# A two-layer graph kernel: the last 255 keys split over both halves of the PE array, key moments from every other row tile, and a narrower test of the candidate pieces

## The chip, the cores and the metric

The kernel runs on one core of one Trainium2 chip. The time is the device time of one execution in microseconds (us), as the median of three runs. Five engines work side by side, each on its own list of instructions in order: PE (TensorE, matmuls; its weight loads are listed as PEld), DVE (VectorE), ACT (ScalarE), POOL (GpSimd) and SP (SyncE, which here only issues transfers). They wait for one another through semaphores.

## The reference, cut to what matters

There are 3327 nodes with 256 features and a sparse weighted adjacency matrix. Layer 0 does two steps of message passing along two ways and adds them up; layer 1 is a graph attention over the neighbours. The change lies in layer 0's learned attention, which keeps for each node the largest probabilities that together make 0.9:

```python
def _top_p_attention(X, W1, W2, W3):
    q = X @ W1.T @ W2.T
    k = X @ W3.T
    logits = q @ k.T / TAU
    probs = jax.nn.softmax(logits, axis=-1)
    idx = jnp.argsort(-probs, axis=-1)
    sp = jnp.take_along_axis(probs, idx, axis=-1)
    cs = jnp.cumsum(sp, axis=-1)
    keep_sorted = cs - sp < TOP_P
    ...
    A = probs * mask
    return A / jnp.maximum(A.sum(-1, keepdims=True), 1e-12)
...
for n in range(STEPS):          # STEPS = 2
    A = _top_p_attention(Xa, W1, W2, W3)
    Xf = R @ Xf                 # R: adjacency plus identity, rows divided by their sums
    Xa = A @ Xa
    Z = Z + Xf @ U1[n].T + Xa @ U2[n].T
```

Everything is float32; queries and keys have 64 features.

## The kernel before

The nodes are cut into 26 row tiles of 128 (the last has 127 rows). Two programs are in the kernel. `fast` computes everything under assumptions that it tests at the end; `general` is a slower program that runs afterwards only if a test failed for some row (`bad`, `far`, `again`).

**Keys and queries.** Since a key has 64 features, the keys of one row tile fill only half of the 128 partitions. `half_of` gives a tile its half (`t // 4 % 2`) and its columns in `kt`: groups of four tiles alternate between the halves. `logits(k)` makes 1024 logits of a row tile at a time, 512 on each half of the PE array, as two matmuls (line 845); `k` runs from 0 to 3, and the fourth piece holds the 255 keys that are left, all on the lower half. `exps` (line 856) takes the exponentials on ACT with their sums. The tile `e` has 3328 columns; POOL writes a zero in the last one for each row tile (line 833).

**Moments.** To guess the threshold of a row, the kernel needs mean and variance of its logits. They come from the sum of the keys and of their products, `gk` (64 x 65 on each half). `moments` adds one row tile to it: a PE transpose of the keys (`turn`, line 733), an ACT copy into `kk` (line 737), a PE product with 65 columns (line 742) and two DVE adds (line 754). `keys_summed` puts this chain into the plan; it is called for every row tile in `prepare` (step 0's keys) and in `finish1` (step 1's keys). `gk` is divided by the number of keys (line 1675), and `stats` (lines 769 to 807) makes mean and variance for each row.

**Search.** For each row tile: `guess` gives a first threshold, `count` (line 893, ACT, over all 3327 exponentials) and `step` (POOL, once on DVE in step 1) improve it two or three times, `window` (lines 948 and 953, DVE) takes the eight largest values below an upper bound out of each of 16 pieces of 208, `sort` and `choose` find among these candidates the exact place of the cut, and `drop` (line 1003) clears what lies under the threshold. `attention` then transposes `e` (line 1016), copies it (line 1021) and multiplies (line 1028). `full` is the product with the adjacency matrix (line 1060), whose tiles SP loads into four buffers.

**The test.** `met` holds numbers for each row tile: 0 the sum, 1 the largest of the eighth values of the pieces, 2 how many values of the window are kept, 3 the first value left out, 4 a count of ties. A row fails in `failures` (lines 1337 to 1348) if, among other things, some piece's eighth value is not below the first value left out, since then that piece might hide a ninth that counts.

**Order.** Nothing is run in the order of the source. `Plan.put` takes each piece of work with its engine, an estimated length, a rank, what it needs and which buffers it takes and gives back; `Plan.order` simulates the engines with these lengths and always takes the ready piece of lowest rank, and `issue` writes the instructions out in that order, which then is fixed for each engine. In the preparation POOL turns variances into factors (lines 672 to 675) and copies keys into `kt` (line 1127); ACT applies the relu (line 1104) and copies projections (lines 1123, 1124); PE transposes (line 1109), projects keys and queries (line 1117) and multiplies the sources of the adjacency products (`project_u`, line 1155), which ACT and DVE copy out (lines 1158, 1159). A piece of SP, `spread`, stores step 1's keys as they come, and `fetch_keys` loads them back.

Of the kernel before, what the change touches and what calls it, by code (L numbers as in the profile page):

```python
# [10 lines left out]
F32 = mybir.dt.float32  # L11
# [4 lines left out]
ALU = mybir.AluOpType  # L16
# [3 lines left out]
P = 128  # L20
N = 3327
NT = 26
NP = NT * P
D = 256
DA = 64
# [545 lines left out]
def fast(  # L571
# [18 lines left out]
    V, S, T, GP = nc.vector, nc.scalar, nc.tensor, nc.gpsimd  # L590
# [19 lines left out]
    bad = const.tile([P, STEPS, NT], F32, name="bad")  # L610
# [6 lines left out]
    for k, v in enumerate(QUANTILE[1:3]):  # L617
        GP.memset(adds[:, k : k + 1], v)

    def half_of(t):  # L620

        r = t // 4 % 2
        lo = t // 8 * 512 + t % 4 * P
        return slice(r * DA, r * DA + DA), slice((1 - r) * DA, (2 - r) * DA), slice(lo, lo + P)

    with ExitStack() as l0:
        wpool = l0.enter_context(tc.tile_pool(name="wpool", bufs=1))
        small = l0.enter_context(tc.tile_pool(name="small", bufs=2))
# [10 lines left out]

        c = wpool.tile([P, NT, D], F32, name="c")  # L640

        kt = wpool.tile([P, 4 * 512 - 256], F32, name="kt")
        qq = wpool.tile([P, NT, P], F32, name="qq")

        kks = [wpool.tile([P, P + 2], F32, name=f"kk{k}") for k in range(2)]
        for kk in kks:
            GP.memset(kk[:, :: P + 1], 1.0)
        wqk = wpool.tile([P, 2, 2, P], F32, name="wqk")
# [7 lines left out]

        stat = wpool.tile([P, 2, NT], F32, name="stat")
        sig, zadd, cn, cs = (wpool.tile([P, NT], F32, name=n) for n in ("sig", "zadd", "cn", "cs"))
        met = wpool.tile([P, 5, NT], F32, name="met")
        GP.memset(met, 1.0)  # L660

        def measure(src):
# [61 lines left out]

        def moments(t, kq, ps_k, ps_g):

            r, p = t // 4 % 2, min(P, N - t * P)
            half = slice(r * DA, r * DA + DA)
            held = {}

            def turn():
                held["ps"] = ps_k()
                T.transpose(held["ps"][:, :P], kq(), ident)

            def copy():
                kk = held["kk"] = kks[t % 2]
                S.copy(kk[:, 1 : P + 1], held["ps"][:, :P])

            def product():
                kk = held["kk"]  # L740
                ps = held["ps"] = ps_g()
                T.matmul(
                    ps[:, : DA + 1], kk[:p, 1 : P + 1], kk[:p, r * (DA + 1) : (r + 1) * (DA + 1)], start=True, stop=True
                )

            def gather():
                for to, src in (
                    (gk[half, :DA], held["ps"][half, 1 - r : DA + 1 - r]),
                    (gk[half, DA : DA + 1], held["ps"][half, DA * r : DA * r + 1]),
                ):  # L750
                    if t in (0, 4):
                        V.tensor_copy(to, src)
                    else:
                        V.tensor_add(to, to, src)

            return turn, copy, product, gather
# [59 lines left out]
        class Row:  # L816


            NAMES = (
                "b v w t0 t1 t2 u g k2 p0 p1 p2 p3 j0 j1 j2 j3 r0 s0 s1 s2 B0 B1 B2 q d dt least up h0 h1 room K zs nxt cnt m "  # L820
                "tk rec".split()
            )

# [3 lines left out]
            def open(self):  # L827
                self.e = epool.tile([P, NP], F32, name="e")
                self.sc = small.tile([P, len(self.NAMES)], F32, name="sc", bufs=BUFS["sc"])
                for k, name in enumerate(self.NAMES):  # L830
                    setattr(self, name, self.sc[:, k : k + 1])
                self.s = met[:, 0, self.i : self.i + 1]
                GP.memset(self.e[:, N:], 0.0)

            def logits(self, k):

                if k == 0:
                    self.open()
                pl = ps_l.tile([P, 2, 512], F32, name="pl")
                w = min(1024, N - 1024 * k)  # L840
                for r in range(2):
                    m = min(512, w - 512 * r)
                    if m > 0:
                        half = slice(r * DA, r * DA + DA)
                        T.matmul(  # L845
                            pl[:, r, :m],
                            qq[half, self.i, :],
                            kt[half, 512 * k : 512 * k + m],
                            start=True,
                            stop=True,  # L850
                        )
                self.pl[k] = pl.rearrange("p r w -> p (r w)")[:, :w]

            def exps(self, k):
                pl = self.pl.pop(k)
                S.activation(  # L856
                    self.e[:, 1024 * k : 1024 * k + pl.shape[1]],
                    pl,
                    AF.Exp,
                    accum_out=(self.p0, self.p1, self.p2, self.p3)[k],  # L860
                )
# [232 lines left out]
        def prepare(t, load):  # L1094
# [19 lines left out]
            def project():  # L1114
                ps = held["ps"] = ps_x.tile([P, P], F32, name="px")
                for k in range(2):
                    T.matmul(
                        ps, wqk[:, k, t // 4 % 2, :], c[:, t, k * P : (k + 1) * P], start=(k == 0), stop=(k == 1)
                    )

            def share():
# [7 lines left out]
            def double():  # L1129
# [9 lines left out]
            a = plan.put("ACT", 0.55, r, share, needs=[a], take=["kq"], give=["px"])  # L1139
            k = plan.put("POOL", 0.35, r, keys, needs=[a])  # L1140
            q = plan.put("SP", 0.2, r, double, needs=[a])
            g = keys_summed(
                t, lambda: held["kq"], lambda: ps_a.tile([P, P], F32, name="acca"),
                lambda: ps_a.tile([P, DA + 1], F32, name="accf"), r, [a], ("acca", "accf"), [],
            )
            plan.put("SP", 0.02, r, lambda: None, needs=[k, q, g], give=["kq"], lag=0.0)
            return [k, q], g

# [13 lines left out]
        def finish1(row, done, rank):  # L1162
# [15 lines left out]
            def project():  # L1178
                ps = held["ps"] = ps_x.tile([P, P], F32, name="px")
                for k in range(2):  # L1180
                    T.matmul(ps, wqk[:, k, t // 4 % 2, :], held["xt"][:, k, :], start=(k == 0), stop=(k == 1))

            def share():
                held["kq"] = small.tile([P, P], F32, name="kq", bufs=BUFS["kq"])
# [37 lines left out]
            if direct:  # L1222
# [2 lines left out]
                    plan.put("POOL", 0.4, r, queries, needs=[a, drawn[0]]),  # L1225
                ]
            kq.append(plan.put("SP", 0.3, r, spread, needs=[a, drawn[0] if direct else None]))
            g = keys_summed(
                t, lambda: held["kq"], lambda: ps_x.tile([P, P], F32, name="px"),
                lambda: ps_x.tile([P, DA + 1], F32, name="px"), r, [a, guessed[0]], ("px", "px"), [],  # L1230
            )
            plan.put("SP", 0.02, r, lambda: None, needs=[kq, g], give=["kq"], lag=0.0)
            a = plan.put("PE", 1.75, r + 0.1, project_u2, needs=[x_], take=["px"])
            a = plan.put("ACT", 0.56, r + 0.1, stage, needs=[a], take=["ystage"], give=["px", "xt"])
# [4 lines left out]
        def fetch_keys():  # L1239
            for r in range(2):  # L1240
                half = slice(r * DA, r * DA + DA)
                w = max(half_of(t)[2].stop for t in range(LAST + 1) if t // 4 % 2 == r)
                nc.sync.dma_start(kt[half, :w], kts[half, :w])
            nc.sync.dma_start(qq[:, : LAST + 1, :], qqs[:, : LAST + 1, :])

# [85 lines left out]
        def failures(n):  # L1331

            b, one = bad[:, n], small.tile([P, NT], F32, name="one", bufs=1)
            W = WIN[n]
            V.tensor_scalar(b, met[:, 2], W / 2, None, ALU.subtract)
            V.tensor_mul(b, b, b)
            V.tensor_scalar(b, b, (W / 2 - 0.5) ** 2, None, ALU.is_gt)
            V.tensor_tensor(one, met[:, 1], met[:, 3], ALU.is_ge)  # L1340
            V.tensor_add(b, b, one)
            V.tensor_scalar(one, met[:, 4], 0.0, None, ALU.not_equal)
            V.tensor_add(b, b, one)
            V.tensor_scalar(one, met[:, 0], 1e-25, None, ALU.is_ge)
            V.scalar_tensor_tensor(one, met[:, 0], 1e30, one, ALU.is_le, ALU.mult)
            V.scalar_tensor_tensor(b, one, 0.0, b, ALU.is_equal, ALU.add)

            V.scalar_tensor_tensor(b[:, NT - 1 :], ident[:, P - 1 :], 0.0, b[:, NT - 1 :], ALU.is_equal, ALU.mult)

        def search(row, rank, keys, stats_of, fresh):  # L1350
# [4 lines left out]
            for g in range(2):  # L1355

                def logits(g=g):
                    row.logits(2 * g)
                    row.logits(2 * g + 1)

                a = plan.put(
                    "PE", 2.1 - 0.5 * g, rank - 2.5, logits, needs=[keys, fresh, a], take=["pl", "pl"] + ["e", "sc"] * (1 - g)
                )
                for k in (2 * g, 2 * g + 1):
                    got.append(
                        plan.put("ACT", 1.15 if k < 3 else 0.5, rank - 2.5, row.exps, k, needs=[a], give=["pl"])
                    )
# [303 lines left out]
        for n in range(STEPS):  # L1671
            base = 30.0 * n
            scaled = plan.put(
                "DVE", 0.2, base - 50.0,
                lambda: V.tensor_scalar(gk[:, : DA + 1], gk[:, : DA + 1], 1.0 / N, None, ALU.mult), needs=[sums],
            )
            cuts = (0, 3, NT // 2, NT)
            of = {}
# [104 lines left out]
```

## Time and profile before

| | |
|---|---|
| median of 3 runs | 2272.42 us (2270.28 to 2273.19) |
| profiled execution | 2271.77 us, its span 2269.9 us |
| PE busy | 2207.6 us, 97% of the span |
| DVE, ACT, POOL busy | 1618.2, 1480.0, 915.3 us |
| granted PE clock, mean | 0.992 |

The span runs from the first to the last instruction of the profiled execution. Preparation takes some 60 us, the row tiles of step 0 the time to about 905 us, those of step 1 the time from there to about 1780, and layer 1's attention the rest. A row of the profile names the line of the kernel, the engine and the tiles written and read (`pl<-kt,qq`). A float32 matmul shows up as two records[...].

### The profile page before, as it was taken

To read this page: it belongs to the slowest core of one execution; us is meant where nothing else is said; L and a number is where in the kernel's file an instruction comes from. 1 tells how busy PE (TensorE), PEld (TensorE's weight loads), DVE (VectorE), ACT (ScalarE), POOL (GpSimd) and SP (SyncE) were. 2 spreads that over 40 slices of the span, in tenths; PEclk is the share of its full clock that TensorE was granted. 3 is DMA by queue.
4 is the path that set the end of the run, shared out by engine and by line. 5 is a ranking of instruction groups with operands and counts; after the bars stand their busy time and mean duration, and the time that the engine had idled before them with its cause. 6 is when DMAs were issued, how large, how long until landed. Compare 5 with 4: busy or idle time off the path is not lost. (4 is left out here: it accounts for less than half of the span.)

```text
span 2269.9 us, 36125 instructions
## 1 busy us (share of the span) xinstructions
PE 2207.6 (97%) x11956; PEld 1547.5 (68%) x11956; DVE 1618.2 (71%) x4273; ACT 1480.0 (65%) x2849; POOL 915.3 (40%) x2263
## 2 busy tenths in 40 slices
PE   7999999999999999999999999999999999999997
PEld 5477778777877778877878777878788433343332
DVE  5576656557565562277878898678776898989895
ACT  5766686677666851478887877777872646565553
POOL 6455555546533540256646656665561000000000
PEclk9999999999999999999999999999999999999998
DMA  3011221212212222531222122222222443434341
GB/s 98 20 37 53 83 69 53 64 51 61 74 48 74 69 82 76 183 86 54 65 57 73 56 61 70 70 75 75 67 74 78 119 118 107 120 106 120 102 126 42
DMA packets 189653, 176.96 MB, mean 78 GB/s; under 512 B 14866, under 2 KB 145808, under 8 KB 189328
## 3 DMA queue, kind: packets, MB, share of 16 engines
q1 hardware_dynamic: 187472, 173.30, 26.3%
q8 instruction: 96, 1.57, 0.3%
q10 hardware_dynamic: 1984, 1.26, 0.2%
q14 instruction: 101, 0.83, 0.1%
HBM read 157.66 MB, written 15.89 MB: 76 GB/s over the span
## 5 line engine op out<-in xcount | busy, mean ns | idle before, releaser
L1028 PE MATMUL acca<-rhs,et 128*128 128x256 f32 x2704 | 621.2, 380 | 0.8 <-ACT et L1021 0.8
L893 ACT ACTIVATE junk<-e,sc 128x3327 fp8e5<-128x3327 f32 x182 | 559.1, 3072 | 59.1 <-POOL sc L938 57.8
L1028 PEld LDWEIGHTS acca<-rhs,et 128*128 128x128 f32 x2704 | 498.5, 190 | 63.8 <-ACT et L1021 2.6
L1060 PE MATMUL accf<-main,at 128*128 128x257 f32 x1352 | 314.0, 382 | 4.9 <-DMA at<-in_adjt_dram 4.6
L1060 PE MATMUL accf<-c,at 128*128 128x256 f32 x1352 | 313.4, 382 | 4.8 <-ACT f L1067 4.7
L1535 DVE SCALAR_TENSOR_TENSOR e<-c,low,et 128x832 f32<-128x832 f32 x288 | 289.0, 1076 | 16.3 <-ACT e L1605 9.7
L1060 PEld LDWEIGHTS accf<-c,at 128*128 128x128 f32 x1352 | 250.2, 190 | 54.8 <-issue 14.1
L1060 PEld LDWEIGHTS accf<-main,at 128*128 128x128 f32 x1352 | 250.7, 191 | 47.1 <-issue 8.2
L1021 ACT COPY et<-px 128x512 f32<-128x512 f32 (+1 forms) x364 | 193.6, 553 | 133.3 <-PE acca L1028 72.5
L948 DVE SCALAR_TENSOR_TENSOR y<-e,sc 128x1664 f32<-128x1664 f32 x104 | 206.6, 1987 | 96.3 <-POOL sc L935 63.8
L953 DVE MAX8 cands<-y 128x8 f32<-128x208 f32 x832 | 242.7, 361 | 3.7
L1003 DVE SCALAR_TENSOR_TENSOR e<-e,thr 128x832 f32<-128x832 f32 x208 | 212.6, 1080 | 1.7
L1551 PE MATMUL pl<-e,main 128*64 128x416 f32 x1152 | 212.0, 516 | 0.1
L856 ACT ACTIVATE e<-pl 128x1024 f32<-128x1024 f32 x208 | 179.1, 863 | 45.6 <-PE pl L845 45.3
L1016 PE MATMUL px<-ident,e 128*128 128x128 f32 x1352 | 193.5, 275 | 7.6 <-ACT et L1021 4.5
L1524 ACT ACTIVATE et<-at 128x512 bf16<-128x512 f32 (+1 forms) x208 | 114.5, 550 | 127.6 <-DVE e L1535 82.4
L1016 PEld LDWEIGHTS px<-ident,e 128*128 128x128 f32 x1352 | 160.4, 141 | 51.6 <-issue 12.5
L845 PE MATMUL pl<-kt,qq 64*128 64x512 f32 (+1 forms) x728 | 184.1, 588 | 0.1
L1551 PEld LDWEIGHTS pl<-e,main 128*64 128x64 f32 x1152 | 79.8, 137 | 122.2 <-issue 102.2
L1535 DVE SCALAR_TENSOR_TENSOR rhs<-c,low,et 128x832 f32<-128x832 f32 x128 | 129.2, 1073 | 0.0
L845 PEld LDWEIGHTS pl<-kt,qq 64*128 64x128 f32 x728 | 70.9, 185 | 82.3 <-issue 76.5
L1523 ACT ACTIVATE at<-at 128x512 f32<-128x512 f32 (+1 forms) x208 | 112.1, 539 | 4.3 <-DMA at<-in_adjt_dram 4.2
(486 smaller groups left out, 2834.3 us busy)
## 6 DMA issues: line engine op xcount, KB each, us to landing
at<-in_adjt_dram SPq DMA_DIRECT2D x416, 256.0 KB, 2.7
at<-in_adjt_dram SPq DMA_DIRECT2D x104, 192.0 KB, 3.0
at<-in_adjt_dram SPq DMA_DIRECT2D x52, 128.0 KB, 2.1
ys<-ystage SPq DMA_DIRECT2D x26, 256.0 KB, 2.2
rhs<-in_x_dram SPq DMA_DIRECT2D x26, 128.0 KB, 2.9
ystage<-in_x_dram SPq DMA_DIRECT2D x26, 128.0 KB, 2.0
base<-ys SPq DMA_DIRECT2D x26, 128.0 KB, 2.2
x1s<-ystage SPq DMA_DIRECT2D x26, 128.0 KB, 1.7
```

The lines of the kernel that those rows point to most:

```text
L845: T.matmul(pl[:, r, :m], qq[half, self.i, :], kt[half, 512 * k : 512 * k + m], start=True, stop=True,)
L856: S.activation(self.e[:, 1024 * k : 1024 * k + pl.shape[1]], pl, AF.Exp, accum_out=(self.p0, self.p1, self.p2, self.p3)[k],)
L893: S.activation(junk[:, :N], self.e[:, :N], fn, bias=t, scale=-1.0, accum_out=dst, saturate=False)
L948: V.scalar_tensor_tensor(self.y[:, : hi - lo], self.e[:, lo:hi], self.up, self.e[:, lo:hi], ALU.is_lt, ALU.mult, accum_out=(self.h0, self. ...
L953: V.max(self.cands[:, o // PIECE, :], self.y[:, o - lo : min(o + PIECE, hi) - lo])
L1003: V.scalar_tensor_tensor(piece, piece, self.thr[:, o : o + 1], piece, ALU.is_gt, ALU.mult)
L1016: T.transpose(pt[:, k, :], self.e[:, j * P : (j + 1) * P], ident)
L1021: S.copy(self.et[g][:, :m, :], self.pt.pop(g)[:, :m, :])
L1028: T.matmul(self.acc, et[:, j - 4 * g, :], rhs[self.n][:, j, :], start=(j == 0), stop=(j == NT - 1))
L1060: T.matmul(self.acc[:, : self.w], self.at[j // JC][:, j % JC, :], self.src[:, j, : self.w], start=(j == 0), stop=(j == NT - 1),)
L1535: V.scalar_tensor_tensor(held["e"][:, k, :], extra["both"][b % 2][:, k, :], low[:, j, k : k + 1], held["mask"], ALU.max, ALU.mult,)
L1551: T.matmul(q["acc"][a][k * FH : (k + 1) * FH, c, :C], main[:, j, h * FH : (h + 1) * FH], held["e"][:, h, c * C : (c + 1) * C], start=(j == 0),
```

## The change

- The last row tile goes to the other half (`side`), so that of the last 255 keys 128 lie on the lower half and 127 on the upper one. The fourth piece of `logits` becomes two matmuls of 128 and 127 columns, and a third one with a single column, of constants (`none`), gives the last place the logit -32000, whose exponential is zero. The zero that POOL wrote into `e` is left out.
- The moments are summed over the 13 row tiles of even number alone, in both steps, and divided by their 1664 keys.
- The test of a piece fails a row if the eighth value is above the first one left out, or equals it while `m`, the number of ties kept, isn't zero. For this `m` moves into `met`.
- The planner's length for the second half of a row's logits is 1.4 instead of 1.6.

```diff
+    def side(t):
+        return 1 if t == NT - 1 else t // 4 % 2
     def half_of(t):
-        r = t // 4 % 2
-        lo = t // 8 * 512 + t % 4 * P
+        r = side(t)
+        lo = t // 8 * 512 + (t % 4 * P if t < NT - 1 else 0)
...
+        none = wpool.tile([P, P + 2], F32, name="none")
+        GP.memset(none, 0.0)
+        GP.memset(none[DA : DA + 32, :P], 1.0)
+        GP.memset(none[DA : DA + 32, P:], -1.0e3)
...
             def copy():
-                kk = held["kk"] = kks[t % 2]
+                kk = held["kk"] = kks[t // 2 % 2]
...
-                GP.memset(self.e[:, N:], 0.0)
+                self.m = met[:, 5, self.i : self.i + 1]
...
-                w = min(1024, N - 1024 * k)
+                w = 512 if k < 3 else P
                 for r in range(2):
-                    m = min(512, w - 512 * r)
-                    if m > 0:
-                        half = slice(r * DA, r * DA + DA)
-                        T.matmul(pl[:, r, :m], qq[half, self.i, :], kt[half, 512 * k : 512 * k + m], ...)
-                self.pl[k] = pl.rearrange("p r w -> p (r w)")[:, :w]
+                    m = min(w, N - 1024 * k - w * r)
+                    half = slice(r * DA, r * DA + DA)
+                    T.matmul(pl[:, r, :m], qq[half, self.i, :], kt[half, 512 * k : 512 * k + m], ...)
+                    if m < w:
+                        T.matmul(pl[:, r, m:w], none[half, :P], none[half, P : P + w - m], start=True, stop=True)
+                self.pl[k] = pl[:, :, :w]
...
-            g = keys_summed(
+            g = t % 2 == 0 and keys_summed(
...
-            )
+            ) or None
...
-            V.tensor_tensor(one, met[:, 1], met[:, 3], ALU.is_ge)
+            V.tensor_tensor(one, met[:, 1], met[:, 3], ALU.is_gt)
+            V.tensor_add(b, b, one)
+            V.tensor_tensor(one, met[:, 1], met[:, 3], ALU.is_equal)
+            V.tensor_scalar(two, met[:, 5], 0.0, None, ALU.not_equal)
+            V.tensor_mul(one, one, two)
             V.tensor_add(b, b, one)
...
-                    "PE", 2.1 - 0.5 * g, rank - 2.5, logits, ...
+                    "PE", 2.1 - 0.7 * g, rank - 2.5, logits, ...
...
-                lambda: V.tensor_scalar(gk[:, : DA + 1], gk[:, : DA + 1], 1.0 / N, None, ALU.mult), needs=[sums],
+                lambda: V.tensor_scalar(gk[:, : DA + 1], gk[:, : DA + 1], 1.0 / (NT // 2 * P), None, ALU.mult), needs=[sums],
```

## The prediction, made before the changed kernel was run

> **What bounds the kernel now.** I read the page first, then a table by stretches of time, then the PE timeline of single stretches, and the list of waits last.
>
> ```profile
> span 2269.9 us, 36125 instructions
> PE 2207.6 (97%) x11956; PEld 1547.5 (68%) x11956; DVE 1618.2 (71%) x4273; ACT 1480.0 (65%) x2849; POOL 915.3 (40%) x2263
> ...
> 0.00:60.00 60.00, 44.43 (x256) 33.51 (x256) 31.75 (x130) 34.77 (x114) 36.14 (x123) 0.97 0.35 101
> 60.00:120.00 60.00, 54.49 (x164) 24.11 (x166) 31.31 (x121) 43.46 (x90) 28.90 (x72) 1.00 0.03 10
> 120.00:620.00 500.00, 499.28 (x2489) 395.76 (x2488) 316.67 (x951) 344.65 (x616) 266.19 (x632) 1.00 0.21 62
> 1000.00:1400.00 400.00, 392.03 (x1935) 313.74 (x1934) 334.48 (x1070) 320.53 (x545) 253.35 (x610) 1.00 0.22 64
> ```
>
> The columns after the length are busy us of PE, PE weight loads, DVE, ACT and POOL. In the first 60 us nothing is full. From 120 us on PE is busy without a break, while DVE and ACT have a third to a sixth of their time free. So in the two graph steps (up to about 1690 us) a microsecond of PE work is a microsecond of the end, and work taken from DVE, ACT or POOL is worth nothing by itself. At the granted clock of 1.00 no clock gain is to be had. What PE work costs is read from the distance between starts, not from the durations, since matmuls overlap:
>
> ```profile
> 562.74 1.55 PE L845 MATMUL pl<-kt,qq 64*128 64x512 f32 x6
> 564.22 0.44 PE L1172 MATMUL px<-ident,xa 128*128 128x128 f32 x2
> ...
> 568.40 0.27 PE L733 MATMUL px<-ident,kq 128*128 128x128 f32 x1
> 568.51 1.91 PE L1060 MATMUL accf<-main,at 128*128 128x257 f32 x8
> 570.25 0.33 PE L742 MATMUL px<-kk 128*128 128x65 f32 x2
> 570.42 8.04 PE L1060 MATMUL accf<-main,at 128*128 128x257 f32 x36
> 578.30 1.04 PE L1016 MATMUL px<-ident,e 128*128 128x128 f32 x8
> 579.27 1.99 PE L845 MATMUL pl<-kt,qq 64*128 64x512 f32 x8
> 581.18 1.09 PE L1016 MATMUL px<-ident,e 128*128 128x128 f32 x8
> ...
> 583.84 0.60 PE L1016 MATMUL px<-ident,e 128*128 128x128 f32 x4
> 584.28 1.89 PE L1028 MATMUL acca<-rhs,et 128*128 128x256 f32 x8
> ```
>
> A float32 matmul is two records, one per pass. Eight passes over 512 columns, for two halves of the array, take 579.27 to 581.18, or 1.91 us: four pairs of 0.43 and 0.2 for changing the tiling on the way in and out. So the halves run together. The second block of a row, with 255 columns on one half only, takes 562.74 to 564.22, or 1.48 = 2 x 0.43 + 0.2 + 2 x 0.21. A 128-column pass is 0.11 (583.84 to 584.28, four of them).
>
> **Part 1, moments from every other tile.** Each chain dropped is a transpose (L733: 568.40 to 568.51, 0.11 us of PE) and a product (L742: 0.17 until the next start, and the 36 passes behind it take 7.88 instead of 36 x 0.2175 = 7.83, so 0.22 in all), one ACT copy (L737, 0.27) and two DVE adds (L754, 0.22 and 0.15). 13 chains go in each of the two places.
>
> In step 0's row endings (150 to 905 us) PE is the bound: 13 x 0.33 = 4.3 us. The ACT and DVE shares (3.5 and 4.8 us) lie beside full PE: nothing. DVE also stands idle ahead of these adds:
>
> ```profile
> DVE gk L754 <- PE px L742: 103.8, 15, 11.0
> ACT rhs L1104 <- POOL mv L675: 6.4, 13, 0.9
> ```
>
> Half of the 103.8 us goes, but DVE's next piece is behind PE anyhow. I count nothing for it.
>
> In the preparation (0 to 62 us) PE is not full, so the 13 x 0.33 there are not simply gained. The relus are paced by POOL (second line above), whose last deviation starts at 46.97 us. What the change moves shows here:
>
> ```profile
> 59.53 0.33 PE L742 MATMUL accf<-kk 128*128 128x65 f32 x2
> 59.91 1.99 PE L845 MATMUL pl<-kt,qq 64*128 64x512 f32 x8
> 61.82 0.44 PE L742 MATMUL accf<-kk 127*128 127x65 f32 x2
> ...
> 76.61 10.82 PE L1155 MATMUL px<-late,c 128*128 128x512 f32 x24 [1.83 <-DVE c L1159]
> ...
> 119.18 0.60 PE L1016 MATMUL px<-ident,e 128*128 128x128 f32 x4
> ```
>
> The first logits start at 59.91; ahead of them stand 4 of the 26 source products (L1155, 1.72 us each) and 25 moments. In the order of the built changed program, 7 source products, all 13 moments and three of the statistics products (two passes of 0.11 us each) stand ahead of them. The old kernel would reach that state, running densely, at 59.9 + 3 x 1.72 + 0.33 + 0.66 = 66.0. The new one: 20 instead of 14 key copies (L1127, 0.29 us and about 0.06 between) now stand ahead of the last deviation on POOL, so that one starts at 46.97 + 6 x 0.35 = 49.1; its relu, transpose, copy and projection take about 2 us more; and then PE has left, in its order, three source products, two moments, two projections (0.45 each) and the statistics: 5.2 + 0.6 + 0.9 + 0.7 = 7.4. First logits at 49.1 + 2 + 7.4 = 58.5, which is 7.5 us sooner at equal work. From there to the first attention (119.18) PE runs source products with some 5.5 us of waits (1.83 is the largest); row 0 is ready for it at 113, when its last threshold pass (L1003) ends, and moves up with the logits, so the gain survives. The price if that cover fails is these waits doubled: 5.5 us. The three new memsets of POOL (a 128x128 memset is 0.2) lie in its idle 1.68 us before the first deviation: nothing. Without that gap they would delay the relus by 0.5. Bounds for the preparation: 2 (only the late part of the chains) and 10.
>
> The SP queue carries the same transfers as before; in the order of the changed program the key fetch still stands behind the last spread of keys, and the loads of adjacency tiles behind that.
>
> **Part 2, the last 255 keys on both halves.** Per row the two 255-column passes (2 x 0.215 = 0.43) become two paired passes of 128 (2 x 0.11 = 0.22), followed by a matmul of one column that fills the last place. 52 rows. The one-column matmul is the unknown. The nearest row is L742, 65 columns: 0.22 us, the same as 128 columns, though it streams half as many; between its passes it is the weight load that counts. Here a rule of the Trainium skill speaks against the change: "TensorE: Matmul & The Clock Gate", section LDWEIGHTS, says that a load takes as long as its columns (128 over 1.2, 107 ns, whatever the rows), and "TensorEngine Tiling (Array Packing)", Instruction Overhead, that one column costs as much as sixty. By that, two loads of 0.107 for one column eat the 0.21 saved, and the part is worth 52 x 0 = 0. By the trace, L742's 0.22 consists of 0.11 for its own two starts and 0.11 by which the instruction behind is late; in a logits block that second share falls into the 0.09 us that the change of tiling costs on the way out already. So I take 0.11 for the column and 0.10 saved per row: 52 x 0.10 = 5.2 us. Ends: 0, and 8 (0.16 a row). A loss would need the two halves to run one after the other (4 x 0.11 + 0.22 against 0.43: 0.23 a row, 12 us); the block at 579.27 excludes that for 512 columns. ACT reads 256 places instead of 255 (385 ns): nothing. POOL loses 52 memsets of 0.1 us: nothing, POOL is 40% busy.
>
> **Part 3, the test.** Four more DVE instructions of 0.16 to 0.19 us on 26 columns, twice. The first time (864 us) PE runs the second step's adjacency products. The second time (1736 us) the last row is being finished: at worst 0.8 us. I take 0.
>
> **Sum.** 4.3 + 7.5 + 5.2 = 17.0 us. The profiled execution took 2271.8 (1.9 around its span); 2271.8 - 17.0 = 2254.8. The median of the runs lies 0.6 above that execution: 2255.
>
> **The rivals.** (a) The column costs its full two loads: 12 us gained, 2260. For it: the page and L742's equal price for 65 and 128 columns. (b) The start gives nothing beyond what PE no longer does late, because source products keep waiting for ACT and DVE behind the 3.07 us count passes: 2 instead of 7.5, so 2261; with (a) too, 2266. (c) Slower: the list of instructions is ordered by a planner, and every order has changed. The place is the head of SP's queue, where a store of keys that waits for ACT holds up the adjacency loads behind it:
>
> ```profile
> 824.86 4.56 PE L1060 MATMUL accf<-main,at 128*128 128x257 f32 x12 [4.62 <-DMA at<-in_adjt_dram]
> ```
>
> Once in this run PE drained all four buffers (4 x 1.73 us) and waited 4.62. Four more such waits, or 0.7 us in each of the 26 rows, decide: 2271.8 - 17.0 + 5 x 4.6 = 2278. Against it: between 120 and 620 us, with the same stores in front, PE lost 0.7 of 500 us. (d) The change doesn't do what it says: half of the keys give a worse first guess, a row fails the test at the end, and the general program computes everything again. Its 27 bisection passes over 52 row tiles, two 1664-column scans of 2.0 us each, alone would be 5.5 ms, so 7.8 ms or more. Against it: the formulas worked out in float32 on the reference's inputs put the kept count between 2 and 26 of 32 in step 1 and between 1 and 22 of 24 in step 0, both inside the windows; in step 1 one row has its eighth largest of a piece equal to the first value left out, which the old test would have failed and the new one lets pass.
>
> **How the numbers follow.** A change under 0.2% (4.5 us) can hardly be told from none with this kernel. Forecast as summed, give or take 5: 0.55. (a): 0.15. (b), alone or with (a): 0.15. Larger gain, because the wait at 824.86 also goes (4.6): 0.05. (c): 0.08, of which half is only an evening out. (d): 0.02. The range 2244 to 2267 holds the forecast, its 8 and 10 us ends, (a) and (b), and leaves out (c), (d) and what is beyond. Faster 0.90, same 0.05, slower 0.05.
>
> **What would show it.** Right: first logits near 58.5 us with seven L1155 tiles ahead; the second logits block 1.38 from start to next start; 26 instead of 52 L742 products; PE as full as now between 120 and 620. Wrong: a block still at 1.48 (the column costs all), first attention later than 113 us, or waits of L1060 for adjacency tiles in many places.

## The result, and the profile after

The changed kernel takes 2261.94 us (median of 4 runs, 2261.57 to 2263.11), against 2271.69 of the kernel before (4 runs, 2270.28 to 2273.19). The ratio is 0.9958, 95% interval 0.9941 to 0.9975: a gain of 9.8 us between the medians, 9.4 between the two profiled spans, where 17.0 had been forecast.

The page of the changed kernel, its span and the busy times:

```profile
span 2260.5 us, 36244 instructions
PE 2194.7 (97%) x12086; PEld 1553.2 (69%) x12086; DVE 1615.3 (71%) x4229; ACT 1470.5 (65%) x2823; POOL 918.3 (41%) x2214
```

PE's busy time fell by 12.9 us, the span by only 9.4: PE stands idle for 3.5 us more than before. A table by stages says where. The stretches of each kernel are: to the first transpose of the first row's attention; row tiles 0 to 22 of step 0; row tiles 23 to 25 with the passage to step 1 and the first row's attention there (called the boundary from here on); step 1 to its last attention product; layer 1. The columns after the length are busy us (and instructions) of PE, PE weight loads, DVE, ACT and POOL, then the granted clock, the DMA share and GB/s. First the kernel before, then the changed one:

```profile
0.00:119.18 119.18, 98.10 (x412) 56.97 (x413) 62.74 (x249) 77.67 (x201) 64.42 (x193) 0.99 0.19 56
119.18:806.80 687.62, 686.19 (x3410) 542.19 (x3409) 426.10 (x1271) 470.87 (x843) 350.67 (x868) 1.00 0.21 61
806.80:1009.30 202.50, 196.06 (x956) 159.10 (x955) 84.22 (x323) 93.45 (x169) 59.85 (x149) 0.99 0.38 115
1009.30:1749.10 739.80, 729.21 (x3614) 591.46 (x3613) 598.86 (x1910) 556.83 (x946) 438.46 (x1050) 1.00 0.23 67
1749.10:2269.90 520.80, 498.02 (x3570) 197.75 (x3568) 446.25 (x521) 281.24 (x691) 1.85 (x5) 0.98 0.37 107
```

```profile
0.00:112.03 112.03, 91.98 (x385) 52.31 (x386) 59.01 (x223) 74.42 (x188) 61.49 (x185) 1.00 0.20 60
112.03:795.20 683.17, 680.31 (x3466) 545.03 (x3464) 424.16 (x1249) 462.89 (x830) 344.28 (x845) 1.00 0.22 61
795.20:1001.80 206.60, 197.88 (x969) 161.86 (x968) 86.69 (x324) 96.49 (x173) 62.97 (x151) 0.98 0.37 112
1001.80:1742.10 740.30, 730.48 (x3718) 599.47 (x3717) 599.15 (x1914) 555.54 (x941) 447.73 (x1031) 1.00 0.24 68
1742.10:2260.50 518.40, 494.06 (x3554) 194.48 (x3552) 446.30 (x521) 281.19 (x691) 1.86 (x5) 0.98 0.37 106
```

The preparation is 7.15 us shorter, rows 0 to 22 are 4.45 shorter, and **the boundary is 4.1 longer**: PE's idle time there (length less busy time) grew from 6.44 to 8.72 us, and the clock fell from 0.99 to 0.98. In step 1 the changed kernel has 16 more adjacency passes (16 x 0.217 us) done before its last attention product, which leaves fewer behind it, so the last two stretches are read together: 1.9 us shorter. -7.15 - 4.45 + 4.1 - 1.9 = -9.4.

The PE timeline of the changed kernel, for the steps of the prediction (start, length, instruction, and in brackets how long PE stood idle ahead of it and for whom):

```profile
58.81 0.83 PE L780 MATMUL px<-gk,qq 128*128 128x129 f32 x6
59.58 1.99 PE L855 MATMUL pl<-kt,qq 64*128 64x512 f32 x8
...
72.97 7.40 PE L1168 MATMUL px<-late,c 128*128 128x512 f32 x16 [1.84 <-DVE c L1172]
...
112.03 0.60 PE L1029 MATMUL px<-ident,e 128*128 128x128 f32 x4
...
585.92 1.35 PE L855 MATMUL pl<-kt,qq 64*128 64x512 f32 x8
587.11 0.28 PE L863 MATMUL pl<-none 64*128 64x1 f32 x2
587.32 0.44 PE L1185 MATMUL px<-ident,xa 128*128 128x128 f32 x2
```

The first logits start at 59.58, 0.3 us sooner than before, but with more source products already behind them; the first attention starts at 112.03 instead of 119.18. The second block of logits (L855 and the one-column matmul, L863) takes 587.32 - 585.92 = 1.40 us to the next start, where it took 1.48.

The place at which the changed kernel loses, first on PE and then on DVE:

```profile
866.31 0.34 PE L753 MATMUL px<-kk 128*128 128x65 f32 x2
866.48 1.09 PE L1073 MATMUL accf<-main,at 128*128 128x257 f32 x4
869.66 0.63 PE L1029 MATMUL px<-ident,e 128*128 128x128 f32 x4 [2.09 <-DVE gk L765]
870.12 3.19 PE L1041 MATMUL acca<-rhs,et 128*128 128x256 f32 x8
```

```profile
865.65 0.21 DVE L1201 COPY kt<-kq 64x128 f32<-64x128 f32 x1
865.79 0.16 DVE L1350 TENSOR_SCALAR bad<-met 128x26 f32<-128x26 f32 x1
...
869.06 0.16 DVE L1365 SCALAR_TENSOR_TENSOR bad<-ident,bad 128x1 f32<-128x1 f32 x1
869.24 0.28 DVE L765 TENSOR_TENSOR gk<-gk,px 64x64 f32<-64x64 f32 x2
```

Read the two together. PE has made the last moments product of step 0 in a `px` buffer by 866.65. DVE is to add it to `gk` (L765), but the test of step 0 (`failures`, L1350 to L1365) stands ahead of this add in DVE's list and takes from 865.79 to 869.22. Until the add is done the buffer isn't free, and the transposes of the next attention need it: PE waits 2.09 us. The eight attention passes behind it then take 3.19 us, where eight such passes elsewhere take 1.89. In the kernel before, the test stood ahead of the add for the same row tile too, but far from it:

```profile
866.70 0.16 DVE L1348 SCALAR_TENSOR_TENSOR bad<-ident,bad 128x1 f32<-128x1 f32 x1
...
880.45 0.28 DVE L754 TENSOR_TENSOR gk<-gk,px 64x64 f32<-64x64 f32 x2 [3.21 <-PE px L742]
```

There DVE had finished the test at 866.86 and stood waiting for PE (3.21 us in the bracket), since this row tile's product came at 880.08. Now it comes at 866.31 and the test ends at 869.22.

Two smaller waits of the same kind lie in the row endings, also on PE of the changed kernel. Here `window` of a row stands ahead of the add in DVE's list (at the first of them 1.95 us for its bound, L961, and 1.21 for four MAX8, L966):

```profile
204.23 0.63 PE L1029 MATMUL px<-ident,e 128*128 128x128 f32 x4 [1.50 <-DVE gk L765]
...
446.51 0.63 PE L1029 MATMUL px<-ident,e 128*128 128x128 f32 x4 [0.79 <-DVE gk L765]
```

The list of waits sums them up; ahead of it the same line of the kernel before:

```profile
PE px L1016 <- DVE gk L754: 1.1, 2, 0.7
```

```profile
PE px L1029 <- DVE gk L765: 4.4, 3, 2.1
```

### The profile page after: what moved, and what is told of

It reads as the page before. It is cut to its first block, busy times and chain, and to the rows that moved or that the text cites. A ratio compares the mean times of both kernels' runs of the same rounds, so it can differ in the third digit from the quotient of the medians.

```text
span 2260.5 us, 36244 instructions
## 1 busy us (share of the span) xinstructions
PE 2194.7 (97%) x12086; PEld 1553.2 (69%) x12086; DVE 1615.3 (71%) x4229; ACT 1470.5 (65%) x2823; POOL 918.3 (41%) x2214
## 4 chain that ended last, share of the span: by engine, by line
PE 74%; ACT 9%; POOL 7%; DVE 5%; issue 3%; DMA 1%; ACTq 0%; POOLq 0%; DVEq 0%; SPq 0%
PE acca L1041 20%; PE accf L1073 19%; PE pl L1568 12%; ACT junk L906 6%; PE px L1029 6%; PE pl L855 5%; PE acca L1582 3%; PE accf L1582 3%; PE px L1216 2%; POOL sc L919 1%; DVE y L961 1%; PE px L1168 1%; DVE cands L966 1%; PE px L1311 1%; DVE e L1552 1%
## 5 line engine op out<-in xcount | busy, mean ns | idle before, releaser
L961 DVE SCALAR_TENSOR_TENSOR y<-e,sc 128x1664 f32<-128x1664 f32 x104 | 209.1, 2011 | 148.9 <-POOL sc L948 146.7
L966 DVE MAX8 cands<-y 128x8 f32<-128x208 f32 x832 | 242.5, 361 | 3.6
L855 PE MATMUL pl<-kt,qq 64*128 64x512 f32 (+1 forms) x832 | 173.5, 535 | 0.0
L855 PEld LDWEIGHTS pl<-kt,qq 64*128 64x128 f32 x832 | 71.6, 186 | 81.4 <-issue 75.7
```

The source lines that it names most:

```text
L855: T.matmul(pl[:, r, :m], qq[half, self.i, :], kt[half, 512 * k : 512 * k + m], start=True, stop=True,)
L961: V.scalar_tensor_tensor(self.y[:, : hi - lo], self.e[:, lo:hi], self.up, self.e[:, lo:hi], ALU.is_lt, ALU.mult, accum_out=(self.h0, self. ...
L966: V.max(self.cands[:, o // PIECE, :], self.y[:, o - lo : min(o + PIECE, hi) - lo])
```

## The experiments

All are compared with the kernel before on the same chip. "Step 0" in the table runs from the first transpose of its first attention to the end of the boundary, which is the last attention product of step 1's first row; "rest" is what follows of step 1, and layer 1. The lengths are those of one profiled execution.

| kernel | median us | ratio, 95% interval | preparation | step 0 | rest |
|---|---|---|---|---|---|
| before | 2271.69 | | 119.2 | 890.1 | 1260.6 |
| changed | 2261.94 | 0.9958, 0.9941 to 0.9975 | 112.0 | 889.8 | 1258.6 |
| e1 no column | 2259.80 | 0.9939, 0.9926 to 0.9953 | 111.3 | 886.6 | 1258.0 |
| e2 late test | 2259.36 | 0.9939, 0.9925 to 0.9953 | 113.7 | 884.9 | 1257.8 |
| e3 first 13 | 2258.89 | 0.9934, 0.9920 to 0.9947 | 112.3 | 882.6 | 1260.0 |
| e4 test only | 2273.72 | 1.0003, 0.9994 to 1.0011 | 119.9 | 890.6 | 1261.8 |
| e5 logits and test | 2266.71 | 0.9976, 0.9967 to 0.9985 | 120.7 | 887.5 | 1259.4 |
| e6 moments and test | 2257.88 | 0.9934, 0.9921 to 0.9948 | 113.1 | 882.6 | 1261.0 |
| e7 moments in the preparation, and test | 2263.08 | 0.9959, 0.9945 to 0.9973 | 111.8 | 890.4 | 1260.8 |
| e8 e2 and e3 | 2256.36 | 0.9928, 0.9914 to 0.9942 | 112.0 | 883.4 | 1259.1 |
| e9 e8, no column, two exponentials | 2254.46 | 0.9921, 0.9908 to 0.9935 | 111.9 | 881.0 | 1258.4 |

The kernel before ran with them at medians of 2273.47 (e1 to e4), 2272.45 (e5 to e8) and 2272.17 us (e9). Already this table shows the main point: the preparation and the rest gain about what was forecast in the kernels that have the parts concerned, while step 0 of the changed kernel gains 0.3 us.

The theory after the result: PE is the bound; the test stands in DVE's list ahead of the last add to `gk`, which holds a buffer that PE needs, and this eats step 0's gain. The rivals: the column costs as much as it saves; the parts are worth less than forecast; something else in the new order costs the time.

**e1, without the column.** The last piece takes 128 columns on both halves, and the matmul of one column is left out. The last place of `e` then holds the exponential of a padding key's logit, so this kernel leaves the excluded place uncleared.

```diff
-                    m = min(w, N - 1024 * k - w * r)
+                    m = w
...
-                    if m < w:
-                        T.matmul(pl[:, r, m:w], none[half, :P], none[half, P : P + w - m], start=True, stop=True)
```

Expected:

> The changed kernel with its instructions in the same order, but without the one-column matmul: both halves take 128 columns, so the last place holds the logit of a padding key (left out: its exponential is one instead of zero). In the trace of the changed kernel the column puts off the next start by 0.32 - 0.20 = 0.12 us a row. Theory 'PE is the bound in every stage': 52 x 0.12 = 6.4 us less, 2255.5 us. Rival 'in step 1 the search sets the pace and freed PE time is lost there': only step 0's half, 3.2 us less, 2258.7 us. Rival 'the column is hidden under the change of tiling': no change.

The median is 2.1 us under the changed kernel's; between the ratios it is 0.0019, or 4.3 us. The step-0 stretch is 3.2 us shorter, and the block shows the price of the column directly. PE timeline of e1:

```profile
583.71 1.35 PE L855 MATMUL pl<-kt,qq 64*128 64x512 f32 x8
584.99 0.44 PE L1185 MATMUL px<-ident,xa 128*128 128x128 f32 x2
...
1449.58 1.72 PE L1029 MATMUL px<-ident,e 128*128 128x128 f32 x8 [3.04 <-ACT et L1034]
```

Without the column the block takes 584.99 - 583.71 = 1.28 us, with it 1.40: the column costs 0.12. 27 second blocks lie in the stretch of step 0, and 27 x 0.12 is 3.2 us, its gain. The 22 of the rest would make 2.6, of which only 0.7 arrive. PE waits longer for the copy of the transposes at one place of step 1 (3.04 us in the last line; 2.19 in the changed kernel); that is 0.85 of the 1.9 us that are missing, and the remainder isn't explained. The wait at the boundary is there as in the changed kernel (2.10 us): the column isn't what was lost.

**e2, the test behind the last adds.** The test of step 0 needs the last adds to `gk`, so the planner sets it behind them. Nothing else in the program is edited.

```diff
+            last_g = [g for _, g, _ in ends] if n == 0 else None
-            failed.append(plan.put("DVE", 2.2, base + NT, failures, n, needs=[[a for a, _ in found]]))
+            failed.append(plan.put("DVE", 2.2, base + NT, failures, n, needs=[[a for a, _ in found], last_g]))
```

Expected:

> The changed kernel, but the test of step 0 (some fifteen small DVE instructions, 3.4 us) needs the last moment add of step 0, so that it stands behind that add in DVE's list. Theory 'the test stands ahead of the add, the add holds the PSUM buffer that PE waits for, and PE's idle time also halves its clock': the wait of 2.09 us at 869.7 and about 1.5 us of half clock behind it go, 3.6 us less, 2258.3 us. Rival 'chance of the order': another wait takes its place, within 1 us of 2262.

The step-0 stretch is 4.9 us shorter, and all of it lies in the boundary (201.7 instead of 206.6). PE timeline of e2 at the same place:

```profile
867.19 1.09 PE L1073 MATMUL accf<-main,at 128*128 128x257 f32 x4
868.11 1.03 PE L1029 MATMUL px<-ident,e 128*128 128x128 f32 x8
868.98 1.89 PE L1041 MATMUL acca<-rhs,et 128*128 128x256 f32 x8
```

PE's list is that of the changed kernel up to these adjacency passes and nearly the same behind them. There is no wait, and the eight attention passes take 1.89. On DVE the add (first line) now comes ahead of the test (second line):

```profile
867.39 0.28 DVE L765 TENSOR_TENSOR gk<-gk,px 64x64 f32<-64x64 f32 x2 [0.82 <-PE px L753]
...
867.81 0.17 DVE L1350 TENSOR_SCALAR bad<-met 128x26 f32<-128x26 f32 x1
```

The clock belongs to it. The table by stages, for 12 us at this place, first the changed kernel and then e2:

```profile
865.00:877.00 12.00, 9.91 (x52) 8.37 (x51) 4.21 (x20) 3.17 (x7) 0.73 (x1) 0.86 0.15 48
```

```profile
865.00:877.00 12.00, 12.00 (x70) 10.30 (x69) 4.51 (x21) 4.17 (x8) 1.29 (x2) 1.00 0.20 64
```

In the changed kernel the granted clock is 0.86 over these 12 us: one piece of 3.4 us at half clock begins at 870.6, just behind the wait of 2.09. It costs at most 1.7 us, so the wait comes to at most 3.8. The rest of the 4.9 lies near 813 us, where PE waits for adjacency tiles in both kernels (4.70 and 5.19 us): the changed kernel's clock was at half for 6.8 us there, e2's for 3.4, which is worth up to 1.7 us, less the 0.5 by which e2 waits longer. That part is not the test's. The whole run gained less than the stretch: its preparation was 1.7 us longer, and the two ratios' intervals overlap.

**e3, the moments from the first 13 row tiles.** In the row endings of step 0 the tiles 0 to 12 are summed instead of every other one; the sample is another one, of equal size, and the copies still alternate between the two `kk` buffers. The last add then falls into the middle of the step, far from the test.

```diff
-            g = t % 2 == 0 and keys_summed(
+            g = t < NT // 2 and keys_summed(
```

Expected:

> The changed kernel, but in step 0's row endings the moments come from the first 13 row tiles instead of those of even number: the same 13 chains, none of them in the last rows. Theory 'the last chains at the step boundary cost what the prediction missed': 3.6 us less, 2258.3 us, and step 1's statistics are ready before its last keys. Rival 'the chains crowd the first rows, where DVE adds also hold up PE (1.5 us at 204 us)': 1 to 3 us more there, so 2260 to 2262.

Step 0 is 7.2 us shorter than in the changed kernel. The boundary, of e3:

```profile
795.20:994.90 199.70, 194.09 (x964) 159.08 (x963) 86.53 (x321) 93.68 (x169) 60.09 (x141) 0.99 0.38 116
```

It takes 199.7 instead of 206.6 us, with 5.6 instead of 8.7 us of idle time. PE's waits for the adds fall from 4.4 to 1.1 us in all. Moving the add away does what moving the test away does. The 2.0 us by which e3's boundary is shorter than e2's are mostly the wait for adjacency tiles there (3.62 instead of 5.19 us), which the edit was not about.

**e4, the test alone.** The kernel before, with the new test of the pieces (the edit is shown against the kernel before).

```diff
-            V.tensor_tensor(one, met[:, 1], met[:, 3], ALU.is_ge)
+            V.tensor_tensor(one, met[:, 1], met[:, 3], ALU.is_gt)
+            V.tensor_add(b, b, one)
+            V.tensor_tensor(one, met[:, 1], met[:, 3], ALU.is_equal)
+            V.tensor_scalar(two, met[:, 5], 0.0, None, ALU.not_equal)
+            V.tensor_mul(one, one, two)
```

Expected:

> The kernel before with the new test alone (four more DVE instructions in each step and the tie count kept in met); moments from all tiles, 255 keys on one half, the old planner length. Theory 'the test's four instructions matter only where they stand in front of a moment add that PE waits for': at the boundary 0.75 us of DVE time and with it up to 1 us more, 2271.7 to 2272.7 us. Rival 'the test costs nothing': 2271.7 us. If it costs 3 us or more, the test is what ate the missing gain.

1.0003 over 13 runs: the four instructions cost nothing where the next product of moments comes 13 us behind the test. By themselves their 0.75 us don't cost; what costs is where the whole test of 3.4 us stands. In the changed kernel's order at most 0.75 of the 2.09 us waited are theirs.

**e5, the logits and the test.** The moments are again summed over all tiles in both places.

```diff
-            g = t % 2 == 0 and keys_summed(
+            g = t < NT and keys_summed(
...
-                lambda: V.tensor_scalar(gk[:, : DA + 1], gk[:, : DA + 1], 1.0 / (NT // 2 * P), None, ALU.mult), needs=[sums],
+                lambda: V.tensor_scalar(gk[:, : DA + 1], gk[:, : DA + 1], 1.0 / N, None, ALU.mult), needs=[sums],
```

Expected:

> The kernel before with the last 255 keys on both halves, the new test and the new planner length; moments from all 26 tiles. By the trace of the changed kernel a row's second block is 0.08 us shorter (1.48 to 1.40). Theory 'PE sets the pace in step 0 and the search in step 1': 26 x 0.08 = 2.1 us from step 0 and up to 0.5 from step 1, ratio to before 0.9989. Rival 'PE sets it everywhere': 4.2 us, 0.9982. The preparation stays at 119 us to the first attention transpose.

The median gain is 5.7 us, with an interval of 3.4 to 7.5. It holds the 4.2 us of the rival, 52 blocks at 0.08 us, and leaves out the 2.6 of the theory. The profiled execution of this kernel was the slowest of its eleven, so its row in the table shows only 2.2 us.

**e6, the moments and the test.** Every other tile in both places; the logits, the layout of the keys and the planner's length as before.

```diff
-                w = 512 if k < 3 else P
+                w = min(1024, N - 1024 * k)
...
-                    "PE", 2.1 - 0.7 * g, rank - 2.5, logits, ...
+                    "PE", 2.1 - 0.5 * g, rank - 2.5, logits, ...
```

Expected:

> The kernel before with the moments from every other tile in both places and the new test; the 255 keys on one half, the old planner length. Theory: first attention transpose about 112 us (7 us sooner), 11 x 0.33 = 3.6 us less in rows 0 to 22 of step 0, step 1 unchanged; at the boundary up to 4 us more if the test again stands in front of the last moment add. Ratio 0.9953 without that loss, 0.997 with it.

14.6 us faster than the kernel before by the medians, interval 11.8 to 18: by the medians a part of the change alone gains more than the whole, though the two intervals still touch (0.9948 and 0.9941). The first two lines are DVE of e6, the next two its PE:

```profile
854.48 0.16 DVE L1360 SCALAR_TENSOR_TENSOR bad<-ident,bad 128x1 f32<-128x1 f32 x1
...
867.08 0.28 DVE L761 TENSOR_TENSOR gk<-gk,px 64x64 f32<-64x64 f32 x2 [3.21 <-PE px L749]
```

```profile
866.71 0.33 PE L749 MATMUL px<-kk 128*128 128x65 f32 x2
866.88 0.60 PE L1024 MATMUL px<-ident,e 128*128 128x128 f32 x4
```

The last product comes at 866.71, close to where it comes in the changed kernel, but in this order the test is over at 854.64. DVE stands ready for the add, and PE loses nothing. The boundary takes 201.0 us. The moments' step 0 is worth 7.5 us here, more than the forecast 4.3; two waits for adds (1.1 us) that the kernel before had are gone too. The remaining 2.1 aren't explained; the five executions of this kernel lie up to 3.3 us apart.

**e7, the moments of the preparation only.** In the row endings all 26 tiles are summed again (the line below is the one there); the logits are as before, and the new test is in.

```diff
-            g = t % 2 == 0 and keys_summed(
+            g = t < NT and keys_summed(
```

Expected:

> The kernel before with every other tile's moments in the preparation alone (all 26 in step 0's row endings) and the new test. Theory 'the preparation gives 7 us and the later stages keep it': 7 us less, ratio 0.9969. Rival 'the gain of the preparation is only the late chains' PE work': 2 us, 0.9991.

The preparation is 7.4 us shorter, the other two stretches are as in the kernel before (+0.3 and +0.2): what the start gains arrives at the end. By the medians it is 9.4 us, interval 6.1 to 12.5, which holds the 7.4.

**e8, e2 and e3 together.** Both edits as above.

Expected:

> Both repairs together: moments of step 0's row endings from the first 13 tiles, and the test needing the last of these adds. With the first alone the add is long done when the test comes, so the second adds a need that is already met. Theory 'one cause, removed twice': as the first alone, ratio 0.993 to 0.994. Rival 'two causes': another 2 us less, 0.9925.

Its interval overlaps that of e3 almost wholly, and holds the rival's 0.9925 too, so the ratio alone decides nothing. The stretch does: step 0 is 0.8 us longer than e3's, not 2 shorter. Two cures of one wait don't add up, as they would if they cured two. Compared with the changed kernel this order takes 6.4 us off step 0, though the moments are of another sample.

**e9, a version without the column's price.** e8, with the matmul of one column left out and the zero in the last place written by POOL as in the kernel before. ACT takes the exponentials of the last piece in two instructions of 128 and 127 columns, so that the padding key is not read. The planner's lengths follow (0.85 for ACT, 1.3 for PE).

```diff
-                    if m < w:
-                        T.matmul(pl[:, r, m:w], none[half, :P], none[half, P : P + w - m], start=True, stop=True)
...
+                    for r in range(2):
+                        lo = 1024 * k + w * r
+                        m = min(w, N - lo)
+                        S.activation(self.e[:, lo : lo + m], pl[:, r, :m], AF.Exp, accum_out=(self.p3, self.p4)[r])
```

Expected:

> Moments from the first 13 tiles and the late test as in the run with both repairs, and no one-column matmul: ACT takes the last 255 exponentials in two pieces of 128 and 127 instead (one more activation of about 0.28 us and one more read of its sum, 0.20), POOL writes the last zero as in the kernel before. PE loses 0.12 us a row, ACT gains some 0.5 us a row. Theory 'PE in step 0, search in step 1': 2 to 3 us less than with both repairs, ratio 0.9915 to 0.992. Rival 'ACT's half microsecond lengthens the search of step 1': step 1's stretch grows from 740 us by up to 26 x 0.5, ratio 0.994 or more.

2254.46 us, the fastest of all; its interval (0.9908 to 0.9935) lies below that of the changed kernel. Against e8 the difference lies within the intervals. ACT's extra work does not show: step 1 and layer 1 are 0.7 us shorter than e8's, not longer, although 8 adjacency passes (8 x 0.217 us) that e8 runs in the stretch of step 0 stand there in e9.

What was not tried: to take away the wait of 3.6 to 5.2 us for adjacency tiles near 813 us, which stands in every kernel here.

## Why the prediction was right on the direction and wrong on the size

**What bounds the kernel: right for step 0.** PE work taken out of step 0 shows in the end where nothing stands in its way (e3, e6, e8), and e4's added DVE work does not show.

**Moments in the preparation: right, in part by luck.** 7.5 us forecast, 7.15 measured, 7.4 in e7. The first logits start at 59.58, not at 58.5: against the 66.0 of equal work that is 6.4 us, and the forecast's agreement with 7.15 to the half microsecond rests on a remainder that it did not name. The visible gain lies between the first logits and the first attention, which took 59.3 us and now 52.5, since seven instead of four source products are already done (3 x 1.72 = 5.2 us). "The gain survives" held; the waits for the copies of source products stayed as large as before (1.84 the largest).

**Moments in the row endings: right by price, lost by order.** 13 x 0.33 = 4.3 us, and step 0's share of the logits, 26 x 0.10 = 2.6, made 6.9 us for step 0. Measured: 0.3. With the same amount of work in another order: 7.5 (e3, of which 1.0 is a shorter wait for adjacency tiles) and 6.7 (e8). So the prices of the sum were nearly sound, and what failed is the step that costed the waits.

**Logits: 0.08 us a row, not 0.10.** The block takes 1.40 us, not 1.38, since the column costs 0.12. That makes 4.2 instead of 5.2 us over 52 rows. The five kernels with the new logits and their column (changed, e2, e3, e5, e8) have a mean rest of 1259.0 us, the four with the old ones (before, e4, e6, e7) 1261.1: 2 us for the 22 second blocks there, where 22 x 0.08 is 1.8. e1's 0.7 of 2.6 does not fit that, so how much of PE's time in step 1 is a microsecond of the end stays open. The rule of the Trainium skill that the prediction brings against the edit ("TensorE: Matmul & The Clock Gate", section LDWEIGHTS) would have made the gain 0; the trace decides for 0.08.

**The test: the step that failed.** "The first time (864 us) PE runs the second step's adjacency products. I take 0." The named cover was the wrong thing to look at. PE did run adjacency products, four passes of them from 866.48, and then it needed a buffer that DVE would free only behind the test. I looked at what PE does while DVE tests, and not at what stands behind the test in DVE's list. In the kernel before nothing urgent was there: the next add came 13 us later. In the changed kernel the product of that row tile moved forward from 880.08 to 866.31 (11.6 of these 13.8 us are what the stretches ahead had gained), while the test, which needs the search of all rows, ended at 869.22 instead of 866.86. The forecast's "Half of the 103.8 us goes, but DVE's next piece is behind PE anyhow. I count nothing for it" failed in the same way. DVE's idle time ahead of the adds did fall (to 49.5 us), and PE's waits for the adds rose from 1.1 to 4.4. But the amount of this idle time isn't what decides: e6 has 42.3 us of it and no such wait. The order does. The third term set at nothing was the clock ("no clock gain is to be had"): it could be lost.

These terms are of the size of what was missed. Step 0 fell short of 6.9 by 6.6 us. PE's waits for the adds grew by 3.3. The changed kernel has 10.2 us of half clock in this stretch and the kernel before 3.4 (at 825.62); the 6.8 more cost at most 3.4. Of the whole, e2 recovers 4.9, the test's part of it being at most 3.8.

**The rivals.** The time, 2262, is close to those of (a), 2260, and (b), 2261, but the profile excludes both: the block is at 1.40 and not 1.48, and the first attention is at 112.0 where (b) wanted at least 117. A time alone would have confirmed the wrong story. That the time lies in the range at all owes much to these two rivals, for which the range was made wide; it is outside the "as summed, give or take 5". (c) did not come (its sum, besides, reckons five more waits where its sentence speaks of four): the wait for adjacency tiles is there once, as before. (d) did not either.

**What stays open.** The medians of e5 and e6 gain 5.7 and 14.6 us, 20.3 together, while e8, which has both in a good order, gains 16.1. Each of these has an uncertainty of some 3 us, so this is no clear contradiction, but the remainder isn't explained. e2's gain over the changed kernel is seen in the stretch, while the intervals of the whole runs overlap.

## What to carry to other kernels

When an edit moves a product forward, read the list of the engine that consumes it: what stands ahead of the consumer there, even if it is harmless today, is what PE will wait for if the consumer frees a PSUM buffer. "Hidden beside PE" is true of a piece of DVE work only if nothing behind it in DVE's list holds something that PE needs soon; look for the next release of a buffer, and not only for the next use of the result. And where a planner fixes the order, build the parts alone as well as together: here one part by itself gained 14.6 us by the medians and the whole 9.8, which no sum of prices can show.

## What the runs showed of the hardware that was not expected

- A wait of PE of 2.09 us was enough for half clock: it is followed by 3.4 us at a granted clock of 0.5, in which the eight passes took 3.19 instead of 1.89 us. In the changed kernel, between 120 and 1740 us, the waits of 4.70, 2.09 and 2.19 us are followed by half clock, and those of 1.50 and 1.18 are not. The length alone doesn't decide: a wait of 2.92 us in e5 and one of 2.35 in e7 were not followed by it. The Trainium skill, "TensorE: Matmul & The Clock Gate", section "HAM oscillation — how this bites in real kernels", puts the limit at idle gaps of over about 3.4 us; by that, only the 4.70 would have been followed. So a short wait for a buffer can cost nearly double (2.09 and up to 1.7 us).
- In these traces what decides is where the wait lies. The half-clock pieces start on a grid: in the changed kernel at 812.54, 870.56 and 1454.24 us, 17 and then 171 times 3.413 us apart, and each lasts one or two such cells. When the eleven traces are cut into these cells (100 to 1740 us), each of the 22 cells at full clock in which PE was idle for 2.09 us or more is followed by half clock, and none with 1.96 us or less is. Below, the first two lines are the changed kernel's cell with the wait of 2.09 us and the cell behind it, the other two the cells that share e5's wait of 2.92. A cell's idle time is its length less PE's busy time, the first figure behind the length; the granted clock is the third figure from the end:

```profile
867.15:870.56 3.41, 1.32 (x9) 0.89 (x8) 2.20 (x13) 0.18 (x2) 0.00 (x0) 1.00 0.47 154
870.56:873.97 3.41, 3.41 (x12) 2.77 (x11) 0.00 (x0) 0.40 (x1) 0.00 (x0) 0.50 0.00 0
```

```profile
1455.62:1459.03 3.41, 2.06 (x10) 1.48 (x8) 0.46 (x2) 2.12 (x1) 2.77 (x10) 1.00 0.62 163
1459.03:1462.44 3.41, 1.84 (x12) 1.68 (x13) 1.98 (x11) 3.38 (x8) 1.38 (x3) 1.00 0.18 68
```

e5's wait is cut into 1.35 and 1.57 us, and the clock stays full. The same grid tells one piece of half clock near 813 us from two: where the wait for adjacency tiles reached 0.70 us or more into the half-clock cell (the changed kernel, e1, e4, e7, e9), a second one followed; where it reached in by 0.26 us or less, none did. So whether a given wait costs its half clock too is in part a matter of its place on this grid, and of luck.
- A matmul of a single column costs 0.12 us behind a block on both halves of the array (1.40 against 1.28 us to the next start), although its two passes start only 0.03 us apart. That is as much as a pass of 128 columns, 0.11, and half of the 0.22 which a 65-column product costs between adjacency passes.
